# Layer 2's first map by seven products in seven of sixteen groups, with the norm prepared three groups ahead

## The chip, the core and the metric

The kernel runs on one core of one Trainium2 chip. The core has TensorE (matrix products), VectorE, ScalarE and POOL (GpSimd) for elementwise work, and queues for DMA, most of them issued by SyncE (SP). The engines run side by side and wait for each other through semaphores. The metric is the device time of one execution in microseconds (us). The kernel before takes 2445.6 us, the median of three runs (2445.13, 2445.6 and 2445.6).

## What is computed

The input x has 128 batches of 64 nodes with 256 features, in float32. Four layers follow one another, each of the form x = x + f(relu(layernorm(x))). Layer 0 is a graph convolution with LSTMs, layer 1 an attention under the graph's mask, layer 3 three graph convolutions. The change is in layer 2:

```
    h = jnp.maximum(_layernorm(x, axis=-1), 0.0)
    ...
        agg = jnp.einsum('nm,bmd->bnd', A_hat, features)
        x = agg.reshape(-1, d)
        h = jax.nn.relu(_batchnorm(x @ W1.T + b1, g1, be1))
        out = h @ W2.T + b2
        out = _batchnorm(out, g2, be2)
```

The 64 nodes are mixed by a 64 x 64 matrix, a first map takes 256 features to 512, a normalization over all 8192 tokens follows, then a relu, a second map from 512 to 256 and another normalization. A normalization over all tokens needs every group's statistics before it can be applied to the first group. A bias that is added ahead of it moves the mean and nothing else.

## The kernel before

The 8192 tokens are cut into 16 groups (g = 0 to 15) of 512 tokens; a tile of a group has 128 partitions. In layer 2 every group owns an "arena", a tile of four slots of 128 x 512. Slots 0 and 1 first hold the normed and rectified tokens (`activated`, L812), tokens along the partitions. `mixed` (L818, helper `mix`, matmuls at L145) mixes the nodes by 64 x 64 matmuls, which also turn the tile, so that slots 2 and 3 hold 256 features by 512 tokens. `hidden` (L822) is the first map: for each of four blocks m of 128 outputs two matmuls (L831) over the two feature blocks into one bank of PSUM, statistics of the result on VectorE (L842, tile `st1`), and a copy with the bias added on ScalarE (L843) into slot m. As m = 2 and 3 are written last, they overwrite the map's own operand.

PSUM has eight banks, given out in turn by `bank`; a mix takes two, a first map four. An engine takes its instructions in the order of the program that a planner writes; `tc.issue_after` puts instructions behind a named one in that order.

Around the loop at L1137 the order is this. The end of attention (L1083 to L1097) already does groups 0 and 1 in part, with the mixes of 0 and 1. Then step g, for g from 2 on, norms group g+1 (statistics L92, aggregates L94, the power -1/2 on POOL at L96, the shift on VectorE at L98, four applications on ScalarE at L111, one for each tile of 128 tokens), mixes group g+1 (one copy on ScalarE, one on VectorE, L158), and does the first map of group g. At g = 3 the second map's weights are fetched into columns 512 to 1024 of the attention's weight tile, which layer 1 has left. The first map's weights lie in columns 0 to 512.

After group 15 `bn_finish` (L1106) makes a scale and a shift for each m from the statistics, with one power on POOL for each, and `activate` (L1224) applies them to a group with the relu. The second map then runs for groups 0 to 3 and 13 to 15 with plain matmuls (L1262), and for groups 4 to 12 by seven products (`second_linear`, L1205, matmuls at L1211).

`seven` (L171) is the helper for a product of 2 x 2 blocks by seven instead of eight block products. Sums of the left blocks (`sums`, L218) and differences of the right blocks (`differences`, L209) are made first. Products 1, 5, 6 and 7 go to four banks; ScalarE copies 1 and 5 out (L180, L181), VectorE adds 6 and 7 to them (L183, L184), POOL adds these two for the last block (L188), and products 2, 3 and 4 are added onto banks that have been read:

```
            products[2](ps[0], False)
            end(0, 0, ps[0])
            products[3](ps[1], False)
            nc.vector.tensor_tensor(out[0][1], p1, ps[1], ALU.add)
            end(0, 1, None)
            products[4](ps[3], False)
```

Product 4 goes to the bank that L184 reads. Layers 0, 1 and 3 use the same helper (matmuls at L569, L881, L1419, L1459 and L1507).

Of the kernel before, what the change touches and what calls it, by code (L numbers as in the profile page):

```python
# [14 lines left out]
P = 128  # L15
# [23 lines left out]
def adj_preln_kernel(ctx: ExitStack, tc: tile.TileContext, x_in, adj, vec, bg0, bg1,  # L39
# [770 lines left out]
    h1s = []  # L810

    def activated(pool, g, between=None):  # L812

        a = arena(pool)
        ln_relu(xs[g], a[:, 0:2, :].rearrange("p a (b d) -> p (a b) d", d=D), between)
        h1s.append(a)

# [20 lines left out]
    def hidden_out(g, ms, pss):  # L838
        a = h1s[g]
        counted = []  # L840
        for m, ps in zip(ms, pss):
            counted.append(nc.vector.bn_stats(st1[:, m, g, :], ps))  # L842
            nc.scalar.activation(  # L843
                a[:, m, :], ps, AF.Identity, bias=vecs[:, V_B1 + m : V_B1 + m + 1]
            )
        return counted

# [4 lines left out]
    with tc.tile_pool(name="att", bufs=2, reuse_waits="tile") as ap_:  # L852
        shifts_made = []

        def normalized(g):
            h = ap_.tile([P, GT, D], F32, tag="h", name="h")
            st, mv, rstd, nmr = (
                lnp.tile([P, GT] + n, F32, tag=t, name=t)
                for t, n in (("st", [6]), ("mv", [2]), ("rstd", []), ("nmr", []))
            )  # L860
            for t in range(GT):
                nc.vector.bn_stats(st[:, t, :], xs[g][:, t, :])
            for t in range(GT):
                nc.vector.bn_aggr(mv[:, t, :], st[:, t, :])
            nc.vector.tensor_scalar(rstd, mv[:, :, 1], LN_EPS, None, ALU.add)
            nc.gpsimd.tensor_tensor(out=rstd, in0=rstd, in1=mhalf, op=ALU.pow)
            nc.vector.tensor_scalar(nmr, mv[:, :, 0], -1.0, None, ALU.mult)
            shifts_made.append(nc.gpsimd.tensor_tensor(out=nmr, in0=nmr, in1=rstd, op=ALU.mult).ins)
            ln_apply(xs[g], h, rstd, nmr)
            return h  # L870
# [114 lines left out]
        def add_output(g, pss, ri):  # L985
            xv = xs[g].rearrange("p t (m q d) -> p (t m) q d", m=2, q=2)
            for par in range(2):
# [4 lines left out]
                nc.gpsimd.tensor_tensor(out=xv[:, :, par, :], in0=xv[:, :, par, :], in1=o, op=ALU.add)  # L992
# [91 lines left out]
        with tc.issue_after(sub):  # L1084
            counted = hidden(0, w1, range(2))
            mixed(1, (on_scalar, on_scalar))
            pss_0 = hidden_products(0, w1, range(2, 4))
# [3 lines left out]
        with tc.issue_after(turned):  # L1091
            ln_apply(xs[2], h1s[2][:, 0:2, :].rearrange("p a (b d) -> p (a b) d", d=D), rstd, nmr)
            counted += hidden_out(0, range(2, 4), pss_0)
        sums_of()
        counted_next = hidden(1, w1, range(2))
# [10 lines left out]
    def bn_finish(st, n, v_0, v_g, v_b, tag, biased=True):  # L1106


        scs, shs = [], []
        for m in range(n):  # L1110
# [11 lines left out]
            if not biased:  # L1122
                nc.vector.tensor_tensor(mean, mean, vecs[:, v_0 + m : v_0 + m + 1], ALU.add)
# [6 lines left out]
            scs.append(sc)  # L1130
            shs.append(sh)
# [4 lines left out]
    behind = [[], [], counted]  # L1136
    for g in range(1, NG):  # L1137
        if g == 1:
            mixed_in = mixed(2, (on_scalar, on_scalar))
            behind.append(counted_next + hidden(1, w1, range(2, 4)))  # L1140
            continue
        if g + 1 < NG:
            with tc.issue_after(behind[g - 1][-1].ins if behind[g - 1] else after_attention):
                pool = ar_right if g + 1 < NG // 2 else keep if g + 1 == NG // 2 else ar_left
                with tc.issue_after(mixed_in):
                    activated(pool, g + 1, (lambda: behind[g][1]) if behind[g] else None)
                mixed(g + 1, (on_scalar, on_vector))
        if g == 3:
            for a in range(2):
                nc.sync.dma_start(  # L1150
                    out=w2[a], in_=w2t.rearrange("(a b p) f -> a p b f", a=2, p=P)[a]
                )
        behind.append(hidden(g, w1))
# [520 lines left out]
```

## Time and profile before

| | |
|---|---|
| median of three runs | 2445.6 us |
| the profiled execution | 2446.36 us |
| its span, first to last instruction | 2444.5 us |
| TensorE busy | 2425.3 us, 99% |
| VectorE, ScalarE, POOL busy | 1539.8, 1127.5, 463.9 us |
| first map L831, 16 groups | 1430.4 us to about 1565 us of the span |
| one step of a group in the middle of the loop | 8.15 us |
| second map by seven products L1211, 9 groups | 54.4 us |

The profile is one execution. A row of a group of instructions gives line, engine, operation, output and inputs, shapes, how many, then the busy time and the mean duration of one in ns, then the idle time of the engine ahead of them and what ended it. A float32 matmul shows as two records, called passes here, each with its own weight load (PEld). The chain is the work that ended last, followed back from the end; in order of time each line is a start, a length and what ran. Durations contain the latency of an instruction, so that two in a row take less than twice one.

### The profile page before, as it was taken

The numbers are of one execution on the slowest core, as the hardware profiler recorded it, in microseconds if no ns is written. First come the engines' busy times: TensorE is split into PE (matmuls) and PEld (weight loads), VectorE is DVE, ScalarE is ACT, GpSimd is POOL, SyncE is SP. The second block draws the span as 40 slices with busy tenths as digits, with TensorE's granted clock in tenths as the row PEclk, the third lists the DMA queues.
The fourth block names the chain that finished last, engine by engine and source line by source line (L and its number), as shares of the span: only waits on it lengthen the run. The fifth ranks groups of instructions, "written<-read, shape, count | busy, mean of one in ns | idle before, by whom it ended". The sixth has DMA issues, their size and how long they took to land.

```text
span 2444.5 us, 46563 instructions
## 1 busy us (share of the span) xinstructions
PE 2425.3 (99%) x19564; PEld 2068.5 (85%) x19564; DVE 1539.8 (63%) x2752; ACT 1127.5 (46%) x2010; POOL 463.9 (19%) x400
## 2 busy tenths in 40 slices
PE   9999999999999999999999999999999999999999
PEld 6678888889999998888888864486988898898888
DVE  6668866666566675575599886476556445454544
ACT  4557754544444443353455566564333323333332
POOL 4432211111111111112224431023111111101110
PEclk9999999999999999999999999999999999999999
DMA  3200000001000000143246410010133100000000
GB/s 128 94 2 1 1 18 1 1 1 35 1 1 1 1 1 1 18 96 70 48 81 128 79 36 2 1 61 10 29 60 62 27 10 19 10 10 10 18 10 18
DMA packets 161585, 73.20 MB, mean 30 GB/s; under 512 B 104416, under 2 KB 157792, under 8 KB 161376
## 3 DMA queue, kind: packets, MB, share of 16 engines
q1 hardware_dynamic: 147712, 56.82, 9.5%
q0 software_dynamic: 12672, 12.58, 3.4%
q8 instruction: 154, 2.52, 0.4%
q10 hardware_dynamic: 992, 0.82, 0.1%
q14 instruction: 55, 0.45, 0.1%
HBM read 40.84 MB, written 20.97 MB: 25 GB/s over the span
## 4 chain that ended last, share of the span: by engine, by line
PE 91%; DVE 5%; ACT 2%; issue 1%; DMA 0%; POOL 0%; DVEq 0%; ACTq 0%; POOLq 0%
PE ps L569 41%; PE ps L1459 16%; PE ps L1507 8%; PE ps L831 4%; PE ps L1419 4%; PE ps L145 4%; PE ps L881 3%; PE ps L512 2%; PE ps L488 2%; PE ps L1211 2%; PE ps L1262 2%; PE ps L903 1%; PE ps L1528 1%; PE ps L964 1%; DVE e L947 1%
## 5 line engine op out<-in xcount | busy, mean ns | idle before, releaser
L569 PE MATMUL ps<-diff,s 128*128 128x256 f32 (+1 forms) x1824 | 393.5, 371 | 0.9 <-DVE diff L690 0.9
L1459 PE MATMUL ps<-arena 128*128 128x256 f32 x1792 | 393.3, 380 | 0.3 <-DVE arena L215 0.3
L1459 PEld LDWEIGHTS ps<-arena 128*128 128x128 f32 x1792 | 337.9, 190 | 55.1 <-issue 9.8
L569 PEld LDWEIGHTS ps<-diff,s 128*128 128x128 f32 x1824 | 345.9, 190 | 33.8 <-issue 1.6
L583 ACT ACTIVATE gates<-gates,lbias 128x512 f32<-128x512 f32 (+5 forms) x426 | 244.3, 621 | 200.5 <-DVE gates L194 144.4
L188 POOL TENSOR_TENSOR gates<-p 128x512 f32<-128x512 f32 (+1 forms) x115 | 148.6, 1292 | 882.0 <-DVE p L184 831.1
L569 PE MATMUL ps<-h,w 128*128 128x256 f32 (+1 forms) x1028 | 241.0, 371 | 0.0
L569 PE MATMUL ps<-diff,w 128*128 128x256 f32 (+1 forms) x1040 | 238.7, 370 | 0.0
L569 PEld LDWEIGHTS ps<-diff,w 128*128 128x128 f32 x1040 | 197.4, 190 | 18.2
L569 PEld LDWEIGHTS ps<-h,w 128*128 128x128 f32 x1028 | 195.0, 190 | 19.2 <-issue 0.5
L583 ACT ACTIVATE gates<-ps,lbias 128x256 f32<-128x256 f32 (+3 forms) x213 | 91.9, 477 | 247.5 <-PE ps L569 247.4
L188 POOL TENSOR_TENSOR arena<-arena 128x256 f32<-128x256 f32 (+1 forms) x73 | 82.2, 1126 | 579.0 <-DVE arena L184 549.3
L238 ACT ACTIVATE arena<-arena 128x512 f32<-128x512 f32 x144 | 88.1, 627 | 187.0 <-POOL arena L188 95.0
L1507 PE MATMUL ps<-arena 128*128 128x128 f32 x1280 | 149.7, 276 | 0.0
L194 DVE TENSOR_TENSOR gates<-p,ps 128x512 f32<-128x512 f32 (+1 forms) x115 | 76.4, 664 | 114.4 <-PE ps L569 114.2
L1507 PEld LDWEIGHTS ps<-arena 128*128 128x128 f32 x1280 | 145.5, 192 | 1.1
L194 DVE TENSOR_TENSOR arena<-arena,ps 128x256 f32<-128x256 f32 (+1 forms) x73 | 43.6, 597 | 156.2 <-PE ps L1459 87.4
L183 DVE TENSOR_TENSOR p<-p,ps 128x512 f32<-128x512 f32 (+1 forms) x131 | 86.9, 663 | 47.9 <-PE ps L569 46.7
L569 PE MATMUL ps<-state,w 128*128 128x256 f32 (+1 forms) x512 | 116.1, 370 | 0.9 <-ACT p L180 0.8
L198 DVE TENSOR_TENSOR gates<-p,ps 128x512 f32<-128x512 f32 (+1 forms) x115 | 76.6, 666 | 63.3 <-PE ps L569 62.7
L831 PE MATMUL ps<-arena,w 128*128 128x512 f32 x256 | 116.0, 606 | 0.0
L569 PE MATMUL ps<-state,s 128*128 128x256 f32 (+1 forms) x512 | 115.8, 369 | 0.0
(207 smaller groups left out, 4012.0 us busy)
## 6 DMA issues: line engine op xcount, KB each, us to landing
x<-in_x SPq DMA_DIRECT2D x19, 512.0 KB, 4.2
y<-turned SPq DMA_DIRECT2D x64, 128.0 KB, 3.6
v<-vt SPq DMA_DIRECT2D x128, 64.0 KB, 2.3
w<-in_wih SPq DMA_DIRECT2D x4, 1024.0 KB, 7.6
x_for_h<-in_x SPq DMA_DIRECT2D x8, 512.0 KB, 7.1
x<-y POOLq DMA_DIRECT2D x8, 512.0 KB, 6.3
x_for_h<-y POOLq DMA_DIRECT2D x8, 512.0 KB, 6.7
z<-w SPq DMA_DIRECT2D x64, 64.0 KB, 2.0
```

The lines of the kernel that those rows point to most:

```text
L145: last = nc.tensor.matmul(pss[b][half * 64 : half * 64 + 64, c, t, :], lhsT=src[rows, t, col : col + 64], rhs=a2[rows, :], start=True, sto ...
L183: nc.vector.tensor_tensor(p1, p1, ps[2], ALU.add)
L188: nc.gpsimd.tensor_tensor(out=out[1][1], in0=p1, in1=p5, op=ALU.add).ins
L194: nc.vector.tensor_tensor(out[0][1], p1, ps[1], ALU.add)
L198: last = nc.vector.tensor_tensor(to, p, q, ALU.add)
L238: nc.scalar.activation(o, o, func)
L569: nc.tensor.matmul(ps[:, r], lhsT=wc[:, j, :], rhs=bc, start=first and r == 0 and c == 0, stop=True, skip_group_check=True,)
L583: nc.scalar.activation(o, ps, func, bias=lbias[:, col : col + 1])
L831: nc.tensor.matmul(ps, lhsT=w1[:, c, m * P : (m + 1) * P], rhs=a[:, 2 + c, :], start=(c == 0), stop=(c == 1),)
L1419: nc.tensor.matmul(ps[:, t, :], lhsT=w[:, t * P : (t + 1) * P], rhs=b, start=first and t == 0, stop=True, skip_group_check=True,)
L1459: nc.tensor.matmul(ps[:, r, :], lhsT=w[:, c, col : col + P], rhs=b[:, c, :], start=first and r == 0 and c == 0, stop=c == 1, skip_group_ch ...
L1507: nc.tensor.matmul(ps[:, t, :], lhsT=w[:, c, t * P : (t + 1) * P], rhs=b[:, c, :], start=first and t == 0 and c == 0, stop=c == 3, skip_gr ...
```

## The change

- Groups 3, 4, 6, 7, 9, 10 and 12 make their first map by seven products (`hidden_seven`), blocks of 256 outputs by 256 features by 256 tokens. The sums of the weight blocks are made once on POOL, behind the last addition of attention, into the columns that the second weights will take; the differences of the mixed features are made by POOL for each of these groups, one step ahead, in two halves of one more arena. The statistics of these groups are taken from the copied result in SBUF.
- The second map's weights are fetched at g = 13, behind the last group of seven products.
- The norm is split: statistics and scale of group g+3 in step g (`scale`), with the shift on POOL (`ln_on_pool`, moved out of attention's `normalized`), and the application of group g+2 in step g (`rectified`), behind the first copies of step g. Group 3's application stands behind the copy of group 1's m = 0.
- Plain groups go through m in the order 2, 3, 0, 1 and write m into slot (m + 2) mod 4, so slots 0 and 1 (the normed tokens, already mixed) are written first. What reads the slots later, the relu, the second map and its blocks, follows this; `bn_finish` goes through m in this order.
- A seven group's mix is copied twice by ScalarE.
- The first map's bias is no longer added by ScalarE; `bn_finish` adds one more small VectorE operation for each m, as it did for the second normalization.

```diff
@@ -807,13 +807,37 @@
...
-    h1s = []
-    def activated(pool, g, between=None):
+    h1s, evicted = [], []
+    FREE_FIRST = (2, 3, 0, 1)
+    def slot(m):
+        return (m + 2) % 4
+    def ln_on_pool(src):
+        st, mv, rstd, nmr = (
+            lnp.tile([P, GT] + n, F32, tag=t, name=t)
+            for t, n in (("st", [6]), ("mv", [2]), ("rstd", []), ("nmr", []))
+        )
+        for t in range(GT):
+            nc.vector.bn_stats(st[:, t, :], src[:, t, :])
+        for t in range(GT):
+            nc.vector.bn_aggr(mv[:, t, :], st[:, t, :])
+        nc.vector.tensor_scalar(rstd, mv[:, :, 1], LN_EPS, None, ALU.add)
+        nc.gpsimd.tensor_tensor(out=rstd, in0=rstd, in1=mhalf, op=ALU.pow)
+        nc.vector.tensor_scalar(nmr, mv[:, :, 0], -1.0, None, ALU.mult)
+        last = nc.gpsimd.tensor_tensor(out=nmr, in0=nmr, in1=rstd, op=ALU.mult)
+        return rstd, nmr, last.ins
+    def activated(pool, g, between=None, scaled=None):
-        ln_relu(xs[g], a[:, 0:2, :].rearrange("p a (b d) -> p (a b) d", d=D), between)
+        dst = a[:, 0:2, :].rearrange("p a (b d) -> p (a b) d", d=D)
+        if scaled:
+            return ln_apply(xs[g], dst, *scaled)
+        ln_relu(xs[g], dst, between)
@@ -840,33 +864,57 @@
...
-            nc.scalar.activation(
-                a[:, m, :], ps, AF.Identity, bias=vecs[:, V_B1 + m : V_B1 + m + 1]
-            )
+            evicted.append(nc.scalar.copy(a[:, slot(m), :], ps).ins)
+    def hidden_differences(g, ts):
+        a = h1s[g]
+        flat = a.rearrange("p c n -> p (c n)")
+        first = flat[:, 2 * GN : 3 * GN].rearrange("p (i n) -> p i n", n=HN)
+        nc.gpsimd.tensor_tensor(out=ts[:, 0:3:2], in0=a[:, 2:4, HN:], in1=first, op=ALU.subtract)
+        nc.gpsimd.tensor_tensor(out=ts[:, 1], in0=a[:, 3, HN:], in1=ts[:, 0], op=ALU.subtract)
+        nc.gpsimd.tensor_tensor(out=ts[:, 3], in0=a[:, 3, 0:HN], in1=ts[:, 1], op=ALU.subtract)
+    def hidden_seven(g, w, ts, copied, added):
+        a = h1s[g]
+        out = [[a[:, 2 - 2 * m : 4 - 2 * m, n * HN : (n + 1) * HN] for n in range(2)] for m in range(2)]
+        b = [[a[:, 2 + c, n * HN : (n + 1) * HN] for n in range(2)] for c in range(2)]
+        def product(wb, x):
+            def issue(ps, first):
+                for r in range(2):
+                    nc.tensor.matmul(
+                        ps[:, r, :], lhsT=wb[:, r * P : (r + 1) * P], rhs=x,
+                        start=first and r == 0, stop=True, skip_group_check=True,
+                    )
+            return issue
+        finish = seven(
+            sevens(w, (*b, [ts[:, i] for i in range(4)]), product),
+            [bank((P, 2, HN)) for _ in range(4)],
+            out[1][0], out[1][1], out, ends_in(out, AF.Copy),
+        )
+        with tc.issue_after(finish.copied):
+            copied()
+        added(finish.behind)
+        finish()
+        return [nc.vector.bn_stats(st1[:, m, g, :], a[:, slot(m), :]) for m in range(4)]
...
         def normalized(g):
...
+            rstd, nmr, made = ln_on_pool(xs[g])
...
@@ -1082,17 +1133,17 @@
-            counted = hidden(0, w1, range(2))
+            counted = hidden(0, w1, range(2, 4))
-            pss_0 = hidden_products(0, w1, range(2, 4))
+            pss_0 = hidden_products(0, w1, range(2))
-            counted += hidden_out(0, range(2, 4), pss_0)
+            counted += hidden_out(0, range(2), pss_0)
-        counted_next = hidden(1, w1, range(2))
+        counted = hidden(1, w1, range(2, 4))
...
-    def bn_finish(st, n, v_0, v_g, v_b, tag, biased=True):
-        scs, shs = [], []
-        for m in range(n):
+    def bn_finish(st, ms, v_0, v_g, v_b, tag):
+        scs, shs = {}, {}
+        for m in ms:
-            if not biased:
-                nc.vector.tensor_tensor(mean, mean, vecs[:, v_0 + m : v_0 + m + 1], ALU.add)
+            nc.vector.tensor_tensor(mean, mean, vecs[:, v_0 + m : v_0 + m + 1], ALU.add)
-            scs.append(sc)
-            shs.append(sh)
+            scs[m], shs[m] = sc, sh
-    behind = [[], [], counted]
+    SEVEN_FC1 = (3, 4, 6, 7, 9, 10, 12)
+    fc1_a = [[w1[:, c, m * D : (m + 1) * D] for c in range(2)] for m in range(2)]
+    fc1_s = [
+        w_att[:, i // 2, 512 + i % 2 * D : 512 + (i % 2 + 1) * D] for i in range(4)
+    ]
+    with tc.issue_after(outputs_added[-1]):
+        sums(nc.gpsimd, *fc1_a[0], *fc1_a[1], *fc1_s)
+    fc1_w = (*fc1_a, fc1_s)
+    fc1_ts = arena(ar_left).rearrange("p i (h n) -> p (i h) n", n=HN)
+    def fc1_t(g):
+        i = SEVEN_FC1.index(g) % 2
+        return fc1_ts[:, 4 * i : 4 * i + 4]
+    counted = [None, counted]
+    scaled = {}
+    def scale(n, behind):
+        if n < NG:
+            with tc.issue_after(behind):
+                scaled[n] = ln_on_pool(xs[n])[:2]
+    def rectified(n):
+        if n < NG:
+            pool = ar_right if n < NG // 2 else keep if n == NG // 2 else ar_left
+            return activated(pool, n, scaled=scaled[n])
+    scale(3, after_attention)
     for g in range(1, NG):
         if g == 1:
-            mixed_in = mixed(2, (on_scalar, on_scalar))
-            behind.append(counted_next + hidden(1, w1, range(2, 4)))
-            continue
-        if g + 1 < NG:
-            with tc.issue_after(behind[g - 1][-1].ins if behind[g - 1] else after_attention):
-                pool = ar_right if g + 1 < NG // 2 else keep if g + 1 == NG // 2 else ar_left
-                with tc.issue_after(mixed_in):
-                    activated(pool, g + 1, (lambda: behind[g][1]) if behind[g] else None)
-                mixed(g + 1, (on_scalar, on_vector))
-        if g == 3:
-            for a in range(2):
-                nc.sync.dma_start(
-                    out=w2[a], in_=w2t.rearrange("(a b p) f -> a p b f", a=2, p=P)[a]
+            mixed(2, (on_scalar, on_scalar))
+            counted[1] += hidden(1, w1, range(2))
+        else:
+            if g + 1 < NG:
+                seven_next = g + 1 in SEVEN_FC1
+                mixed(g + 1, (on_scalar, on_scalar if seven_next else on_vector))
+                if seven_next:
+                    hidden_differences(g + 1, fc1_t(g + 1))
+            if g == SEVEN_FC1[-1] + 1:
+                for a in range(2):
+                    nc.sync.dma_start(
+                        out=w2[a], in_=w2t.rearrange("(a b p) f -> a p b f", a=2, p=P)[a]
+                    )
+            if g in SEVEN_FC1:
+                counted.append(
+                    hidden_seven(
+                        g, fc1_w, fc1_t(g), lambda: rectified(g + 2), lambda last: scale(g + 3, last)
+                    )
-        behind.append(hidden(g, w1))
+                continue
+            pss = hidden_products(g, w1, FREE_FIRST)
+            counted.append(hidden_out(g, FREE_FIRST[:1], pss))
+            with tc.issue_after(evicted[-1]):
+                last = rectified(g + 2)
+            with tc.issue_after(last) if last else nullcontext():
+                counted[g] += hidden_out(g, FREE_FIRST[1:], pss[1:])
+        scale(g + 3, counted[g][2 if g == 1 else 0].ins)
+        if g == 1:
+            with tc.issue_after(evicted[-2]):
+                rectified(3)
-    sc1, sh1 = bn_finish(st1, 4, V_B1, V_G1, V_BE1, "n1")
+    sc1, sh1 = bn_finish(st1, FREE_FIRST, V_B1, V_G1, V_BE1, "n1")
...
-            order = [(c, m) for c in range(4) for m in range(2)]
+            order = [(c, m) for c in FREE_FIRST for m in range(2)]
-                    pss[m], lhsT=w2[c // 2][:, c % 2, m * P : (m + 1) * P], rhs=a[:, c, :],
-                    start=(c == 0), stop=(c == 3),
+                    pss[m], lhsT=w2[c // 2][:, c % 2, m * P : (m + 1) * P], rhs=a[:, slot(c), :],
+                    start=(c == FREE_FIRST[0]), stop=(c == FREE_FIRST[3]),
-            def evicted(m):
+            def evict(m):
...
```

More of the change, by code (lines that the diff above doesn't have):

```diff
@@ L852, in adj_preln_kernel @@
     with tc.tile_pool(name="att", bufs=2, reuse_waits="tile") as ap_:
-        shifts_made = []
+        shifts_made, outputs_added = [], []
         def normalized(g):
             h = ap_.tile([P, GT, D], F32, tag="h", name="h")
[L857 to L868, printed above, removed]
+            rstd, nmr, made = ln_on_pool(xs[g])
             ln_apply(xs[g], h, rstd, nmr)
+            shifts_made.append(made)
             return h
@@ L991, in add_output @@
                 )
-                nc.gpsimd.tensor_tensor(out=xv[:, :, par, :], in0=xv[:, :, par, :], in1=o, op=ALU.add)
+                added = nc.gpsimd.tensor_tensor(
+                    out=xv[:, :, par, :], in0=xv[:, :, par, :], in1=o, op=ALU.add
+                )
+            outputs_added.append(added.ins)
             return last
@@ L1148, in adj_preln_kernel @@
-        if g == 3:
-            for a in range(2):
-                nc.sync.dma_start(
-                    out=w2[a], in_=w2t.rearrange("(a b p) f -> a p b f", a=2, p=P)[a]
-                )
-        behind.append(hidden(g, w1))
+            mixed(2, (on_scalar, on_scalar))
[15 more added lines that the diff above has]
+                        g, fc1_w, fc1_t(g), lambda: rectified(g + 2), lambda last: scale(g + 3, last)
+                    )
+                )
+                continue
[5 more added lines that the diff above has]
+                counted[g] += hidden_out(g, FREE_FIRST[1:], pss[1:])
@@ L1193, in fc2_blocks @@
         return [
-            [a[:, 2 * c : 2 * c + 2, n * HN : (n + 1) * HN] for n in range(2)] for c in range(2)
+            [a[:, 2 - 2 * c : 4 - 2 * c, n * HN : (n + 1) * HN] for n in range(2)]
+            for c in range(2)
         ]
@@ L1220, in second_linear @@
             sevens((*fc2_a, fc2_s), (*fc2_blocks(a), ts), product), [bank((P, HN)) for _ in range(4)],
-            a[:, 0, HN:], a[:, 1, HN:], blocks, ends_in(blocks, AF.Copy),
+            a[:, 2, HN:], a[:, 3, HN:], blocks, ends_in(blocks, AF.Copy),
         )
@@ L1225, in activate @@
         a = h1s[g]
-        for m in range(4):
+        for m in FREE_FIRST:
             nc.scalar.activation(
-                a[:, m, :], a[:, m, :], AF.Relu,
+                a[:, slot(m), :], a[:, slot(m), :], AF.Relu,
                 bias=sh1[m], scale=sc1[m],
@@ L1272, in adj_preln_kernel @@
                 if (g, m) != (NG - 1, 1):
-                    last = evicted(m)
+                    last = evict(m)
             if g + 2 < NG:
@@ L1280, in adj_preln_kernel @@
             w_three = layer3_weights()
-    sc2, sh2 = bn_finish(st2, 2, V_B2, V_G2, V_BE2, "n2", biased=False)
+    sc2, sh2 = bn_finish(st2, range(2), V_B2, V_G2, V_BE2, "n2")
     b1, t1s, a2, s2s, b3, t3s = w_three
@@ L1383, in first_start @@
             normalize(g, chunks=[1], on_scalar=range(2))
-        evicted(1)
+        evict(1)
         lns = []
```

## The prediction

> **What bounds the kernel now.** I read the page's busy row and chain first, then the chain in order of time through layer 2, then TensorE's timeline and the stretches where it is not full, then the groups of the other engines.
>
> ```profile
> PE 2425.3 (99%) x19564; PEld 2068.5 (85%) x19564; DVE 1539.8 (63%) x2752; ACT 1127.5 (46%) x2010; POOL 463.9 (19%) x400
> ...
> PE 91%; DVE 5%; ACT 2%; issue 1%; DMA 0%; POOL 0%; DVEq 0%; ACTq 0%; POOLq 0%
> ```
>
> TensorE sets the end almost everywhere; a TensorE pass removed is a gain only if nothing else becomes late. The chain through the stage that changes (start, length, what):
>
> ```profile
> 1493.23 1.09 PE ps L145 x64
> 1494.32 7.06 PE ps L831 x16
> 1501.39 1.09 PE ps L145 x64
> 1502.48 7.06 PE ps L831 x16
> ...
> 1593.78 54.40 PE ps L1211 x252
> ```
>
> Each group is a mix (L145, 1.09) and the first map (L831, 7.06, 16 passes: eight fp32 matmuls, two records each). A period is 8.155 us, and from 1461 to 1551 nothing but TensorE is on the chain. L1211 is layer 2's second map, already by seven products: nine groups in 54.40 us, 6.04 a group. The entry to the stage is different (first TensorE's timeline, then the stretches around it, with the busy time of TensorE, of its weight loads, of VectorE, ScalarE and POOL; the third figure from the end is the granted clock, 1.00 at full speed):
>
> ```profile
> 1445.14 3.70 PE L831 MATMUL ps<-arena,w 128*128 128x512 f32 x8
> 1449.92 1.92 PE L145 MATMUL ps<-ah,arena 64*64 64x64 f32 x64 [1.09 <-ACT arena L111]
> 1451.78 8.83 PE L831 MATMUL ps<-arena,w 128*128 128x512 f32 x16
> ```
>
> ```profile
> 1443.00:1449.00 6.00, 5.84 (x137) 3.40 (x136) 5.71 (x23) 3.92 (x8) 1.02 (x1) 1.00 0.01 3
> 1449.00:1455.00 6.00, 5.00 (x69) 2.65 (x70) 4.75 (x16) 4.83 (x10) 3.50 (x3) 0.77 0.01 3
> 1455.00:1461.00 6.00, 6.00 (x42) 2.66 (x44) 2.71 (x7) 4.77 (x10) 1.02 (x1) 0.95 0.00 1
> ```
>
> TensorE waits 1.09 us for the norm of group 3 on ScalarE, runs the mix in 1.92 instead of 1.16 because the norm's four tiles come one by one, and then the clock falls: group 2's map takes 8.83 instead of 7.13. Together 3.6 us.
>
> **The change, part by part.**
>
> *Seven products for seven groups (3, 4, 6, 7, 9, 10, 12).* A plain group is 16 passes of 512 columns; their weight loads stand 0.43 apart, so 16 x 0.43 = 6.88, and 0.18 of the 7.06 goes where TensorE changes between 64-row and 128-row tiles. A group of seven is 14 matmuls of 256 columns, 28 passes. The same shape runs in L1211 at 54.40 / 252 = 0.2159 a pass: 28 x 0.2159 = 6.04. With all 0.18 of the tile change kept it is 6.22, with none 6.04; layer 3's L1419 (28 passes of 256 columns) takes 6.13 up to a 64-row matmul. I take 6.18, 0.14 of change. Saved: 7.06 - 6.18 = 0.88 a group, 7 x 0.88 = 6.2 us (ends 5.9 and 7.1).
>
> [...] A load is 190 ns here: 16 x 0.19 = 3.0 of 7.06 us (43%) before, 28 x 0.19 = 5.3 of 6.18 (86%) after. [...] were the loads not hidden, the worst I would allow is the saving gone, 6.2 us lost. The row decides: L1211 holds 0.2159 a pass with loads at 88% (47.8 of 54.4 us).
>
> *Is what surrounds it covered?* The step of a seven group is then 1.09 + 6.18 = 7.27. VectorE in it: four norm statistics (1.39 for x4, 1.31 to the next), four aggregates 0.28, two small ones 0.3, four additions from PSUM and four statistics of 512 columns. The rows of these, with latency:
>
> ```profile
> L842 DVE BATCH_NORM_STATS2 st<-ps 128x6 f32<-128x512 f32 x64 | 44.4, 697 | 43.0 <-PE ps L831 42.4
> ...
> L194 DVE TENSOR_TENSOR arena<-arena,ps 128x512 f32<-128x512 f32 x18 | 12.4, 688 | 38.6 <-PE ps L1459 32.8 <-PE ps L1419 5.9
> ...
> L1254 DVE BATCH_NORM_STATS2 st<-arena 128x6 f32<-128x512 f32 x18 | 12.2, 689 | 0.8
> ```
>
> Two in a row show 1.28 to 1.29, 0.60 each: 8 x 0.60 = 4.8. Sum 1.3 + 0.3 + 0.3 + 4.8 = 6.7, and 0.6 for the mix's copy where a plain group follows: 7.3 against 7.27. A plain step needs 1.9 + 4 x 0.60 = 4.3 against 8.16 and lets it catch up. Three steps (seven, seven, plain): 6.7 + 7.3 + 4.3 = 18.3 of 22.7. Within a pair the tight point is product 4 of the second group, which needs the addition at L184 done. Count from that step's start T. VectorE still holds the first group's last addition (product 4 of it ends at T, so T+0.2 to 0.8), its four statistics (to 3.2) and the copy (3.8). L183 to 4.4; L184 must await product 7 (T+1.2+4 x 0.86 = 4.6) and ends at 5.3. Product 4 is due at T+6.3: 1.0 us spare. ScalarE: four norm tiles 2.0, two copies of the mix 1.1, three of products 1.6, 4.7 of 7.27. POOL: power 1.02, shift 0.20 (the row of the same operation in attention), differences 1.28 + 2 x 0.95 (rows L188 and L215), addition 1.28: 5.7 of 7.27, and the differences are made a whole step ahead, with about 3 us to spare. No stall in steady state, so cost 0.
>
> *Norm steps ahead.* The statistics go to three groups ahead, the norm itself to two, the shift from VectorE to POOL. In the steady state the norm was not late before, so this is worth nothing there. At the entry it is. VectorE's order in the changed program is: statistics of group 3 (as before, 1444.1), aggregates, two statistics of group 1, both attention outputs (2 x 0.60), then group 1's m=0 statistics, at about 1448.3 to 1449.0. ScalarE's copy of that result now stands ahead of group 3's norm (before, the norm started at 1449.25 right behind the mix's copies): copy 1449.05 to 1449.55, first norm tile done at 1450.15. TensorE stands from 1448.84 to 1450.2: 1.35 instead of 1.09. The fourth tile follows a second copy and is done at 1452.1; but one matmul of group 2 now fills the wait for it (TensorE's order puts it between the mix's third and fourth tile). Mix plus that matmul end at 1452.7; before, the same work ended at 1451.84 + 0.86 = 1452.7. Net 0. POOL must make the four weight sums (4 x 0.95) behind attention's last additions (to 1450.3) and ahead of group 4's power: 1454.1 + 1.0 + 0.2 = 1455.4; group 4's norm is due on ScalarE at about 1456.9. Covered by 1.5; if that cover goes, the norm of group 4 has a further 3 us before TensorE's mix.
>
> The clock at the entry: [...] The row shows the clock at 0.77 after a wait of only 1.09 (plus three gaps between tiles). I go by the row: same 1.7 as before, net 0; -1.7 stays as the lower end and +1.7 (a second slow stretch, of the same size) as the upper.
>
> *Free slots first, no bias in the first map.* The copy 0.58 replaces the activation 0.68 on ScalarE, off the path: 0. The second weights now load behind group 12 instead of group 3, on SP; they have two steps (16 us) for two 256 KB transfers (1 MB loads land in 7.6): 0. The first normalization gains one VectorE addition for each of four m, behind the wait for POOL's power. This chain is on the path:
>
> ```profile
> 1567.81 0.62 DVE st L842
> 1568.45 0.60 DVE n1mv L1114
> ...
> 1570.07 0.23 DVE n1sh L1126
> 1570.33 0.82 ACT arena L1227
> ```
>
> In the second normalization, which has that addition, it adds 0.08 between its neighbours. 4 x 0.06 to 0.08 = 0.25 us more before the last activation; TensorE's wait there grows from 0.51 to 0.76 (ends 0 and 0.6).
>
> *Sum.* -6.2 + 0 + 0.25 = -5.95. The profiled execution is 2446.36 with a span of 2444.5: 2440.4 and 2438.55 after. The runs' median stands 0.76 below the profiled time: 2445.6 - 5.95 = 2439.65.
>
> **Rivals.**
>
> *VectorE becomes the bound and the kernel slower.* In the seven groups it goes from 62% (5.1 of 8.15 in one group's stretch) to 92%. For: 17 dependent instructions a step[...]. Against: 1.0 us spare at product 4, and a plain group follows each pair. It decides when VectorE's part of a step passes 7.27 by 0.88, at 8.15 us, which is 22% above my sum. If it came so late that each of the seven groups stood 1.0 us and paid the clock as at the entry, 7 x (1.0 + 1.7) - 5.95 = +13: 2458.5.
>
> *Part of it is given back.* One or two stalls in the three pairs, or at the first seven group, which starts right after the slow stretch; 1.0 us with the clock's 1.7 once: 2442.3. For: the clock's fall after 1.09 us. Against: the spare times above.
>
> *The entry keeps its clock.* 2439.65 - 1.7 = 2438.0. For: [...] that the mix's gap is filled. Against: a longer first wait.
>
> *The change does nothing.* Loads not hidden behind 256 columns: 2445.6 + 0.25 = 2445.8. L1211 speaks against.
>
> **How the numbers follow.** Likeliest (net of the sum) 0.58, 2439.65, its own range 2438.0 to 2441.0: the ends of its terms (-7.1 and -5.3), widened by 0.5 and 0.7 for the entry. Given back in part 0.20. Entry keeps its clock 0.10. Nothing 0.05. Slower 0.07. The 0.2% bound, about what a measurement of this kernel can tell from no change, is 4.9 us: 2440.7 and 2450.5. Likeliest lies below 2440.7 for 0.52 of its 0.58; with 0.10 and 0.02 of the partial case: faster 0.64, same 0.29, slower 0.07. The range 2437.2 to 2443.4 leaves out half of "nothing" upward, all of "slower" and the tails.
>
> **What would show it.** Right: the product line in the first map has 196 passes in 7 x 6.2 us; the step of a seven group is 7.2 to 7.3; TensorE has no idle time at product 4; the clock falls once, near 1450; the last activation of the first normalization follows the group's end by 0.2 more. Wrong: waits of TensorE on L184's addition or on POOL's differences, a clock below 1.00 between 1461 and 1545, or an entry more than 1 us later than before at the end of group 2 (1460.6).

## The result, and the profile after

The changed kernel takes 2441.26 us (median of 22 runs, 2439.79 to 2443.13), the kernel before 2445.16 us beside it (22 runs, 2443.99 to 2446.73): ratio 0.9983, interval 0.9978 to 0.9989. That is 3.9 us or 0.16% faster, a real gain, but under the 0.2% that the prediction called measurable. It lies inside the predicted range, 1.6 us above the predicted time and just above the likeliest case's own range (2438.0 to 2441.0): of the 5.95 us forecast a third is missing. The profiled executions show more: 2446.36 and 2441.49 us, spans 2444.5 and 2439.7. What they show is told first, and then why it is not the usual difference.

The busy row and the chain by engine, from the page of the changed kernel:

```profile
PE 2419.9 (99%) x19648; PEld 2084.9 (85%) x19648; DVE 1552.0 (64%) x2777; ACT 1121.7 (46%) x2010; POOL 497.5 (20%) x445
...
PE 92%; DVE 5%; ACT 2%; issue 1%; POOL 0%; DMA 0%; ACTq 0%; DVEq 0%; POOLq 0%
```

TensorE still sets the end; it does 84 more passes and is busy 5.4 us less (1.7 us of this is the clock of one execution, below). The chain of the changed kernel in order of time, in the middle of the stage (start, length, what):

```profile
1482.42 1.09 PE ps L145 x64
1483.51 6.24 PE ps L888 x28
1489.75 1.09 PE ps L145 x64
1490.84 6.24 PE ps L888 x28
1497.08 1.09 PE ps L145 x64
1498.17 7.06 PE ps L855 x16
```

A group by seven products (L888) takes 6.24 where a plain one (now L855) takes 7.06; nothing but TensorE is on the chain. The only waits of TensorE from 1430 to 1570 us are at the entry and behind the first normalization:

```profile
PE ps L145 <- ACT arena L111: 1.4, 1, 1.4
PE ps L1354 <- ACT arena L1319: 0.6, 1, 0.6
```

The entry, first TensorE's timeline (in brackets the wait ahead and whose result ended it) and then the stretches around it (the third figure from the end is the granted clock):

```profile
1445.43 3.70 PE L855 MATMUL ps<-arena,w 128*128 128x512 f32 x8
1450.50 1.45 PE L145 MATMUL ps<-ah,arena 64*64 64x64 f32 x48 [1.37 <-ACT arena L111]
1451.87 1.12 PE L855 MATMUL ps<-arena,w 128*128 128x512 f32 x2
1452.93 0.46 PE L145 MATMUL ps<-ah,arena 64*64 64x64 f32 x16
1453.32 6.28 PE L855 MATMUL ps<-arena,w 128*128 128x512 f32 x14
```

```profile
1443.00:1449.00 6.00, 6.00 (x138) 3.39 (x136) 5.97 (x18) 4.06 (x9) 1.94 (x3) 1.00 0.01 3
1449.00:1455.00 6.00, 4.57 (x71) 2.46 (x71) 4.30 (x13) 4.25 (x9) 5.71 (x9) 1.00 0.01 3
1455.00:1461.00 6.00, 6.00 (x77) 3.09 (x76) 4.21 (x14) 4.24 (x9) 3.94 (x5) 1.00 0.00 1
```

TensorE waits 1.37 us, 0.28 longer than before, and one matmul of group 2 (two passes) stands between the mix's third and fourth tile, all as forecast; but the clock stays at 1.00 where before it fell to 0.77. VectorE's rows in the stage, from 1461 to 1545 us:

```profile
L904 DVE BATCH_NORM_STATS2 st<-arena 128x6 f32<-128x512 f32 x28 | 17.3, 679 | 0.0
...
L184 DVE TENSOR_TENSOR arena<-arena,ps 128x512 f32<-128x512 f32 x7 | 4.8, 689 | 1.0 <-PE ps L888 0.7
```

At L184, the tight point of the prediction, it is VectorE that waits for TensorE and not the other way; in every group by seven L184 ends 0.77 us before product 4 starts. The end of the first normalization on the chain:

```profile
1561.24 0.62 DVE st L866
1561.88 0.60 DVE n1mv L1165
1562.51 0.17 DVE n1sc L1166
1562.74 0.56 POOL n1sc L1167
1563.32 0.16 DVE n1sc L1174
1563.48 0.08 DVE n1mv L1173
1563.59 0.23 DVE n1sh L1176
1563.84 0.82 ACT arena L1319
```

The added operation is the 0.08 at L1173, four times. From the last product on the chain to the last activation it was 10.12 us before (1560.21 to 1570.33) and is 10.40 (1553.44 to 1563.84).

### The profile page after: what moved, and what is told of

Read it like the earlier page. It is cut to its first block, busy times and chain, and to the rows that moved or that the text cites. A ratio compares the mean times of both kernels' runs of the same rounds, so it can differ in the third digit from the quotient of the medians.

```text
span 2439.7 us, 46858 instructions
## 1 busy us (share of the span) xinstructions
PE 2419.9 (99%) x19648; PEld 2084.9 (85%) x19648; DVE 1552.0 (64%) x2777; ACT 1121.7 (46%) x2010; POOL 497.5 (20%) x445
## 4 chain that ended last, share of the span: by engine, by line
PE 92%; DVE 5%; ACT 2%; issue 1%; POOL 0%; DMA 0%; ACTq 0%; DVEq 0%; POOLq 0%
PE ps L569 41%; PE ps L1551 16%; PE ps L1599 8%; PE ps L145 4%; PE ps L1511 4%; PE ps L929 3%; PE ps L512 2%; PE ps L488 2%; PE ps L1303 2%; PE ps L855 2%; PE ps L888 2%; PE ps L1354 2%; PE ps L951 1%; PE ps L1620 1%; PE ps L1012 1%
## 5 line engine op out<-in xcount | busy, mean ns | idle before, releaser
L1551 PE MATMUL ps<-arena 128*128 128x256 f32 x1792 | 393.4, 381 | 0.4 <-issue 0.4
L1551 PEld LDWEIGHTS ps<-arena 128*128 128x128 f32 x1792 | 337.8, 190 | 55.4 <-issue 10.8
L188 POOL TENSOR_TENSOR arena<-arena 128x512 f32<-128x512 f32 (+1 forms) x80 | 90.8, 1134 | 598.5 <-DVE arena L184 598.5
L194 DVE TENSOR_TENSOR arena<-arena,ps 128x512 f32<-128x512 f32 (+1 forms) x80 | 48.1, 602 | 155.5 <-PE ps L1551 87.4
L183 DVE TENSOR_TENSOR arena<-arena,ps 128x512 f32<-128x512 f32 (+1 forms) x80 | 48.1, 602 | 106.7 <-PE ps L1551 53.5
```

What stands on the lines that cost most here:

```text
L183: nc.vector.tensor_tensor(p1, p1, ps[2], ALU.add)
L188: nc.gpsimd.tensor_tensor(out=out[1][1], in0=p1, in1=p5, op=ALU.add).ins
L1551: nc.tensor.matmul(ps[:, r, :], lhsT=w[:, c, col : col + P], rhs=b[:, c, :], start=first and r == 0 and c == 0, stop=c == 1, skip_group_ch ...
```

## Theory and rivals

To find the missing third I cut every trace at the same points of TensorE's timeline: the *stage*, from the first map's first product to the end of the 12 second-map passes that run ahead of TensorE's wait for the normalization; the second map's nine groups of sevens; and *layer 3*, from its first product at L1459 (changed kernel L1551) to the start of TensorE's last group. The starting point of the stage itself moves by up to 2.5 us between runs (1430.3 to 1432.8), so lengths are compared and not times of day.

The first runs ask about the clock. Theory A: its fall in the first profile of the kernel before (8.83 instead of 7.13) was an accident of that execution; theory B: it belongs to every run of that kernel. The later ones ask where the rest went. My theory: the sevens give what they seem to give; the rest of the change costs something at the entry and at the normalization, and something is lost far behind the stage. Rivals: the sevens save less than they seem to, because something else becomes late, or VectorE is nearly the bound.

## The experiments

**Both kernels once more.**

> The kernel before, unchanged, profiled a second time. Its first profiled execution (2446.36) lay 1.2 above its median of 22 runs (2445.16), and lost 1.7 us to a fallen clock in group 2's map. Theory A, the fallen clock at the entry is a matter of luck and the usual run doesn't have it: group 2's map takes about 7.1 instead of 8.8 us, and the time is near 2444.7. Theory B, the entry always loses the clock after its wait of 1.09: 8.8 again.

> The changed kernel, unchanged, profiled a second time. In its first profile the wait at the entry was 1.37 us and the clock was kept (group 2's map 1.12 + 6.28 for 16 passes). Theory A: kept or lost by luck; if lost, group 2's map and mix end some 1.7 us later. Theory B': the changed entry keeps it always because a matmul fills the mix's last gap: the same as in the first profile. Steps of seven groups 7.33 us both ways.

Measured 2445.49 and 2441.06 us. TensorE's timeline of the kernel before, second profile:

```profile
1450.67 1.93 PE L145 MATMUL ps<-ah,arena 64*64 64x64 f32 x64 [1.08 <-ACT arena L111]
1452.53 7.13 PE L831 MATMUL ps<-arena,w 128*128 128x512 f32 x16
```

The same wait, the same gaps between tiles, and no fall: 7.13 instead of 8.83. The 1.7 us of the first profile is not in this execution, whose time lies at the median, so B falls as an "always"; the fall came again in a later profile (six small matmuls, below). The changed kernel repeats its first profile: a wait of 1.38 us, the clock kept. With the clock kept on both sides the stage is 138.55 before and 133.39 after, 5.16 less. The table has the lengths of all runs in us, by the starts and ends in TensorE's timeline. The stage runs from the first product of the first map to the end of the 12 passes of the second map ahead of the wait for the normalization (for instance 1558.41 + 5.72 - 1430.74 = 133.39), layer 3 from the first L1551 (before: L1459) to the start of the last row of L1620 (before: L1528):

| run | stage | second map, sevens | layer 3 | median |
|---|---|---|---|---|
| before, first profile | 140.24 | 54.56 | 746.65 | 2445.16 |
| before, again | 138.55 | 54.56 | 746.72 | |
| before, wait filled | 138.55 | 54.56 | 746.72 | 2444.94 |
| before, 6 small matmuls | 140.24 | 54.56 | 748.55 | 2447.11 |
| after, first profile | 133.39 | 54.94 | 746.91 | 2441.26 |
| after, again | 133.39 | 54.94 | 747.42 | |
| after, wait filled | 133.74 | 54.95 | 748.52 | 2442.78 |
| after, 3 small matmuls | 133.39 | 54.95 | 746.39 | 2440.52 |
| no sevens | 139.16 | 54.94 | 746.39 | 2446.14 |
| ten sevens | 130.92 | 54.95 | 746.03 | 2437.71 |
| norm of group 3 earlier | 132.46 | 54.94 | 747.30 | 2439.64 |
| statistics twice | 142.39 | 54.94 | 746.40 | 2448.76 |
| eleven sevens, norm earlier | 130.78 | 54.93 | 746.02 | 2436.24 |
| ten sevens, norm earlier | 129.99 | 54.94 | 745.95 | 2436.39 |

**The wait at the entry filled with a matmul**, in both kernels (a first product made twice, for m = 3 before and m = 1 after):

```diff
-            for c in range(2):
+            for c in (0, 0, 1) if (g, m) == (1, 3) else range(2):
...
```

> The kernel before, with one matmul of group 1's last block (m = 3) made twice, 0.86 us of TensorE work put into its wait at the entry. The wait falls from 1.09 to about 0.2. Theory A: if the usual run of before doesn't lose the clock, the median stays within 0.4 us of before. Theory B: the clock is no longer lost and the median falls by 1.5 to 1.7 us.

> The changed kernel with the same extra matmul (group 1's m = 1). The wait falls from 1.37 to about 0.5. If the longer wait of the changed entry costs its usual run the clock (a rival for where 2 us of the forecast went), the median falls by 1.5 us from 2441.3, to about 2439.7; if the usual run keeps the clock, it stays at 2441.3 within 0.4.

Measured 2444.94 us before (ratio 1.0, 0.9991 to 1.0008) and 2442.78 after (0.999, 0.9982 to 0.9998, against the kernel before). In the kernel before TensorE's wait falls from 1.08 to 0.22 and its stage stays at 138.55: the extra matmul exactly takes the wait's place, and the clock is kept. Its median lies only 0.38 us under that of the kernel before beside it (2445.32, 25 runs). If the usual run lost the clock, the fill would have taken 1.5 to 1.7 us out. So theory A holds: the usual run of the kernel before keeps its clock. In the changed kernel the fill made it 1.5 us *slower*, which neither side of the expectation had: two waits at the entry (0.54 and 0.26, stage +0.35), and layer 3, over 200 us further on and untouched, took 1.1 to 1.6 us longer. That was the first sign of a cost that no part of the change accounts for.

**Without the sevens; with ten of them.**

```diff
-    SEVEN_FC1 = (3, 4, 6, 7, 9, 10, 12)
+    SEVEN_FC1 = ()                        # one run, without the weight sums on POOL
+    SEVEN_FC1 = tuple(range(3, 13))       # the other
```

> The changed kernel with no group by seven products: all fourteen later groups plain, the rest of the change (norm steps three groups ahead, outputs in the slots that are free first, bias left to the batch norm) kept. Theory (the sevens save 0.82 us each on TensorE, and the rest of the change costs about 1 us): 7 x 0.82 = 5.8 us more than the changed kernel, 2447.0 (2446.3 to 2447.7), slower than the kernel before by 1 to 2 us; each step of the stage 8.15 us. Rival (the sevens save less than they seem to, since something else waits): 2442 to 2444.5.

> The changed kernel with ten groups by seven products, 3 to 12, with no plain group between. Theory (TensorE bounds the step at 7.33 us, VectorE at some 6.7 fits under it): three more steps of 7.33 instead of 8.15, 2.5 us less than the changed kernel, 2438.8 (2438.0 to 2439.5), no wait of TensorE inside the stage. Rival (VectorE or the buffers bound sevens that follow one another): waits of TensorE ahead of a mix or inside the products, 0.5 us or more per step, 2441 to 2445.

Measured 2446.14 us (ratio 1.0004, 0.9996 to 1.0012) and 2437.71 (0.9967, 0.9955 to 0.998). The stage is 5.77 longer without sevens and 2.47 shorter with three more: 0.82 a group both ways, as in the chain. Ten in a row run with no wait of TensorE between them; VectorE is busy 6.74 to 6.75 of each step, the 6.7 of the prediction's sum (three successive steps; VectorE is the third of the engine figures):

```profile
1475.00:1482.33 7.33, 7.33 (x93) 6.26 (x92) 6.74 (x19) 4.82 (x9) 5.23 (x6) 1.00 0.01 2
1482.33:1489.67 7.34, 7.34 (x94) 6.27 (x93) 6.75 (x19) 4.82 (x9) 5.23 (x6) 1.00 0.01 2
1489.67:1497.00 7.33, 7.33 (x94) 6.26 (x93) 6.75 (x19) 4.82 (x9) 5.24 (x6) 1.00 0.00 0
```

The first rival falls. Both times are about 1 us under the expectation and just outside its range; both runs have a shorter layer 3 (746.39 and 746.03). The run without sevens also prices the rest of the change in the stage: 139.16 - 138.55 = 0.61 us *lost*.

**VectorE loaded.** The four statistics of a seven group are made twice.

```diff
         finish()
+        for m in range(4):
+            nc.vector.bn_stats(st1[:, m, g, :], a[:, slot(m), :])
         return [nc.vector.bn_stats(st1[:, m, g, :], a[:, slot(m), :]) for m in range(4)]
```

> The changed kernel with the four batch statistics of each group by seven products made twice (2.7 us more on VectorE in each of seven groups). Theory (TensorE bounds a pair and the plain group behind it at 22.8 us; VectorE has 18.3 us of work in them, which becomes 23.7): TensorE waits 0.9 us or more per pair, more where a buffer is held, up to 1.9 us per seven: 2444 to 2454, with waits whose releaser is VectorE. Rival (VectorE isn't near the bound): less than 1 us more, 2442.2 or under.

Measured 2448.76 us (ratio 1.0016, 1.0009 to 1.0022), the stage 9.0 longer. TensorE's waits in the stage:

```profile
PE ps L888 <- DVE arena L184: 3.1, 3, 1.0
PE ps L145 <- ACT arena L111: 2.5, 5, 1.4
```

```profile
1473.16 0.45 PE L145 MATMUL ps<-ah,arena 64*64 64x64 f32 x12
1474.64 1.10 PE L888 MATMUL ps<-arena,w 128*128 128x256 f32 x4 [1.03 <-DVE arena L184]
```

(from the list of waits, us in total, times, longest; and TensorE's timeline). TensorE stops where the prediction put the tight point: product 4 of the second group of a pair, behind L184, in each of the three pairs. The second set of statistics takes 2.46 us; with the 1.0 spare of the prediction product 4 should come 1.46 late. It starts 6.85 us behind the group's first product (1467.79 to 1474.64), in the changed kernel 5.29 (1467.95 to 1473.24), so it comes 1.56 late, and a part of the mix fills 0.45 of that. The place was right, and the spare time is 0.9 instead of 1.0. A pair and its plain group now take 25.47 us instead of 22.82. The rival's deciding point, 8.15 us of VectorE in the step of a group by seven, is passed (6.7 + 2.5 = 9.2), and the gain is indeed gone: three plain steps take 24.5 us. Over the three steps, though, VectorE has only 18.3 + 2 x 2.5 = 23.3 us of work; an average over them would not have shown the loss. Of the 2.65 us a pair, 1.03 is this wait, 0.29 and 0.77 go where the next norm is late and its tiles come to the mix one by one, and the rest with the split mix. What counts is the latest product, not the sum.

**Where the code lies.** A few 64 x 64 matmuls in the wait at the very start, 64 being the smallest operand that the kernel already uses. Their result is used by nothing; they move TensorE's later instructions within the pieces, 154 of 16.4 KB each, that the page's queue of instructions brings (q8, below). At the start they take 0.69 us for three and 1.34 for six (4.33 to 5.67 in the timeline), more than the expectations say.

```diff
             keep_busy(7)
+            for _ in range(3):                 # 6 in the kernel before
+                nc.tensor.matmul(idle[0:64, 0:64], lhsT=ones[0:64, 0:64], rhs=ones[0:64, 0:64],
+                                 start=True, stop=True)
```

> The changed kernel with three matmuls of 64 x 64 more in the wait at the very start (12 instructions of TensorE, some 0.1 us, in time it waits in anyway). Theory (the waits without a releaser in layer 3, 0.5 us in the third step and 0 to 0.4 in the eleventh, fall where TensorE's instructions cross from one 16 KB piece of code to the next): the pieces now end elsewhere in the steps, these waits go or move, layer 3 from its first product to TensorE's last instruction takes 746.5 us or less instead of 746.9 to 747.4, the time is 2440.2 to 2440.9. Rival (the waits belong to the program's own semaphores): they stay at the same matmuls, 2441.0 to 2441.5.

> The kernel before with six matmuls of 64 x 64 more in the wait at the very start (24 instructions of TensorE, some 0.15 us). Theory of code pieces: this puts the ends of the pieces where they fall in the changed kernel with one extra matmul, which lost 1.9 us in layer 3: layer 3 from its first product to the last instruction of TensorE takes 747.7 to 748.7 us instead of 746.7, with waits without a releaser just behind the small products, the time is 1 to 2 us longer, 2446.2 to 2447.2. Rival: layer 3 as before, 2445.2.

Measured 2440.52 us for the changed kernel (ratio to the kernel before 0.9982, 0.9974 to 0.999) and 2447.11 for the one before (1.0008, 1.0 to 1.0016). Layer 3 is 746.39 and 748.55, both as the theory of code pieces had them: three matmuls at the start took 0.5 to 1.0 us out of the changed kernel's layer 3, and six put 1.8 us into the other's. The chains of the changed kernel (again) and of the kernel before with six small matmuls:

```profile
1778.71 1.90 PE ps L145 x128
1780.61 0.43 PE ps L1620 x8
1781.04 0.84 PE ps L1551 x3
1781.89 0.42 issue
1782.31 1.78 PE ps L1551 x7
```

```profile
1833.99 1.73 PE ps L145 x116
1835.71 0.43 PE ps L1533 x8
1836.15 0.41 PE ps L1464
1836.56 0.77 issue
1837.33 4.69 PE ps L1464 x21
```

"issue" is time in which TensorE waited for nothing that the profile shows. The queue that brings its instructions is, by its count, this one in the page's list of queues (transfers, MB, share), kernel before:

```profile
q8 instruction: 154, 2.52, 0.4%
```

2.52 MB in 154 transfers are 16.4 KB each; in the trace every one has 16384 bytes. TensorE has 39442 instructions in the trace (19564 loads, as many matmuls, 314 others), in the changed kernel 39623 to 155 transfers: 256 to a transfer and 64 bytes each, an estimate by division (256.1 and 255.6). I counted TensorE's instructions up to each load in layer 3 that came late without a releaser: 27073 and 34497 in the changed kernel; 27073, 29889, 34497 and 37313 with the wait filled; 27842 and 35266 in the kernel before with six small matmuls; 32450 without the sevens. Each leaves 193 or 194 when divided by 256. With the filled wait the program is four instructions longer, and the stall stayed at 27073, two passes earlier in layer 3's program. So it belongs to the place in the stream and not to the instruction. That TensorE waits there for its next piece is what the counts point to; no record of the trace names what ended the stall. (In both profiles with small matmuls the stage also began 1 to 2 us later than in most others. With six, two more such stalls stand ahead of it, 0.65 and 0.93 us at 1249.6 and 1308.5, at 194 behind a multiple of 256; with three the delay lies ahead of layer 0's long products.) All in layer 3 stand behind a mix of 128 small passes, which uses up 256 instructions in 1.9 us; 256 instructions of the sevens last 128 x 0.2159 = 27.6 us.

**The norm of group 3 earlier on ScalarE**: straight behind the copies of group 2's mix instead of behind the eviction of group 1's m = 0.

```diff
-            mixed(2, (on_scalar, on_scalar))
+            mixed_2 = mixed(2, (on_scalar, on_scalar))
+            with tc.issue_after(mixed_2):
+                rectified(3)
...
-        if g == 1:
-            with tc.issue_after(evicted[-2]):
-                rectified(3)
```

> The changed kernel with the norm of group 3 given to ScalarE straight behind the copies of group 2's mix, ahead of the eviction that it stood behind. Theory (the entry costs 0.4 us more than before because ScalarE comes to group 2's tiles 0.3 us later, and because a matmul group is put between the mix tiles): TensorE waits 0.9 to 1.1 us at the entry instead of 1.37, stage from its first product to the end of the first map 133.0 instead of 133.4 us; time 2440.4 to 2441.2. Rival (the clock: with the mix tiles together again the fall seen in two profiles of the kernel before comes back): group 2's products take 8.8 us instead of 7.1, stage 134.7.

Measured 2439.64 us (ratio 0.9977, 0.9968 to 0.9986). TensorE's entry:

```profile
1450.28 1.93 PE L145 MATMUL ps<-ah,arena 64*64 64x64 f32 x64 [0.56 <-ACT arena L111]
1452.13 7.13 PE L855 MATMUL ps<-arena,w 128*128 128x512 f32 x16
```

The wait falls to 0.56, below the kernel before, and the planner leaves the mix in one piece; the stage is 0.93 shorter, twice what I expected, and the clock is kept. The changed kernel's entry was late because of one eviction ahead of the norm.

**Together.**

> The changed kernel with eleven groups by seven products, 3 to 13, and the norm of group 3 given to ScalarE straight behind the copies of group 2's mix, ahead of the eviction that it stood behind. Theory: four more sevens save 4 x 0.82 = 3.3 us, and the wait at the entry falls from 1.37 to about 0.9 us: some 3.7 us less than the changed kernel, 2437.5, with layer 3 between 747.3 and 749.8 us by where the code pieces end: 2436.6 to 2438.6. Rival (VectorE at 6.75 us of a step of 7.33 falls behind over eleven steps, or the clock falls at the entry, 1.7 us): waits of TensorE inside the stage, or the first map 1.7 us longer; 2438.6 to 2441.

> The changed kernel with ten groups by seven products, 3 to 12, and the norm of group 3 given to ScalarE straight behind the copies of group 2's mix. Theory (the two gains add, and the late norm of the last group, which made TensorE wait 1.6 us behind the eleventh, stays away): stage from its first product to the end of the first map 133.4 - 0.9 - 2.5 = 130.0 us, no wait of TensorE in it but the 0.56 us at the entry, layer 3 747.3 us as in the runs with ten and eleven; time 2435.5 to 2437.0. Rival (they share a gain, or the wait behind the last one comes with ten as well): stage 130.8 us or more, 2437 or more.

Measured 2436.24 us (ratio 0.9963, 0.995 to 0.9975) and 2436.39 (0.9961, 0.9948 to 0.9975). With eleven, the norm of group 15 comes late and TensorE waits 0.75 us ahead of the last mix, which then takes 1.94 instead of 1.16: the stage is 130.78 where the gains sum to 132.46 - 4 x 0.82 = 129.2. With ten the two gains add to 129.99, as expected. In medians the two can't be told apart; both beat the changed kernel by some 5 us and the kernel before by 0.4%.

## Why the prediction was right and where not

With the clock kept on both sides the lengths account for the gain: stage -5.16, wait behind the normalization +0.07, second map +0.38, layer 3 +0.19 to +0.70. Sum -4.5 to -4.0, beside -3.9 of the medians. Of the 2.05 us that the forecast is short by, 0.43 are the sevens (5.77 instead of 6.2), 0.39 the entry, 0.03 the normalization, 0.38 the second map and 0.19 to 0.70 layer 3.

- *Seven products, 0.88 a group, 6.2 us.* Right in mechanism, a little large. A group takes 6.24 and not 6.18: all of the tile change is kept (6.24 - 6.04 = 0.20), where I had taken 0.14. 7.06 - 6.24 = 0.82; seven times this, 5.77 by the run without sevens, lies just under the lower end of 5.9. 28 loads of 190 ns are 85% of 6.24 us, and in the stage no product of L888 waited for anything; so the row (L1211) and not the load's busy share was the right judge.
- *Is what surrounds it covered.* Right. No wait of TensorE between 1461 and 1544; 6.7 us of VectorE was measured at 6.75, and the 1.0 us spare came out at 0.9 in the loaded run. POOL's sums took 2.92 for four, less than the 3.8 of the estimate.
- *Norm steps ahead, net 0 at the entry.* Wrong by 0.39. The wait grew to 1.37 as forecast (1.35). But I set "mix plus that matmul" equal on both sides with the matmul at 0.86; set between the mix's tiles it has a change of tile shape on either side, and takes 1.06 (1451.87 to 1452.93). From the stage's start to the end of group 2 it is 28.40 before (again) and 28.79 after.
- *The clock at the entry, "same 1.7 as before".* Wrong in this: the row of one execution was taken for the kernel's habit. Its net of 0 for the clock held by luck, because the usual run loses it on neither side. The fall was there in two of three profiles of the kernel before with the wait of 1.08 to 1.09 us, and in none of six of the changed kind with 1.37 or 1.38, so the length of the wait doesn't decide. Its place may. The changes of the clock stand whole multiples of 3.4133 us apart in the traces: in the first profile of the kernel before at 4.97, 1452.22 and 1455.63 us (424 steps and one), in the first of the changed kernel at 9.80 and 2436.68 (711 steps). The program's start lies differently on this grid in the two: 4.97 and 9.80 are 1.4 steps apart. The steps of the grid at the entry, with the products of the first map alone (busy time of TensorE, of its loads, then the clock): the first profile of the kernel before, the step behind it, and the second profile.

```profile
1448.81:1452.22 3.41, 0.47 (x2) 0.30 (x2) 1.00 0.00 0
1452.22:1455.63 3.41, 3.41 (x5) 1.35 (x4) 0.50 0.03 5
1449.73:1453.14 3.41, 0.61 (x2) 0.37 (x3) 1.00 0.00 0
```

In both profiles with the fall (the first, and the one with six small matmuls) one step holds the whole wait and the whole mix, and 0.47 us of products. In the second profile the step begins 0.14 us after the wait does and has 0.61 us; in the six of the changed kind the emptiest has 0.92, all of it the matmul between the tiles. Wait and mix together take 2.94 us, so by these lengths about one position in seven would hold them whole (an estimate, (3.41 - 2.94) / 3.41). That is not far from the 12 of 120 runs of the kernel before that lie more than 1 us above their median, but no run varied the position, so the place is a likely cause and not a shown one. The first profiles' 4.8 us of span are then -5.16 in the stage and -1.69 of clock, +0.71 behind the stage, +0.29 by which the stage began later and +1.08 by which the last output landed later behind TensorE's end.
- *End of the first normalization, +0.25.* Right: +0.28, but only 0.07 of it is in the wait (0.51 to 0.58); 0.21 is in the 12 passes ahead, which wait for single activations (5.51 to 5.72).
- *Behind the stage.* The sum had nothing there; this is the step that failed. Second map: +0.38, in every kernel of the changed kind, with sevens or without. ScalarE's order at the start of the nine groups, changed kernel (again), timeline:

```profile
1587.89 0.58 ACT L1360 COPY arena<-ps 128x512 f32<-128x512 f32 x1 [3.30 <-DVE st L1363]
1588.37 0.38 ACT L180 COPY arena<-ps 128x256 f32<-128x256 f32 x1
1588.64 0.60 ACT L1360 COPY arena<-ps 128x512 f32<-128x512 f32 x1
1589.11 2.94 ACT L1319 ACTIVATE arena<-arena,n1sh,n1sc 128x512 f32<-128x512 f32 x4
```

The copy of a product (L180) has come between the two evictions; before, it stood behind them and the four activations. The loads behind the last activations wait 0.21 and 0.40. Why the planner changed it was not tried. Layer 3: TensorE's program has 168 loads and matmuls and 13 waits more by then, and by the theory of code pieces these end at other places of the steps: 0.53 more was measured in the third step in both profiles and 0.45 in the eleventh in one. In the last step L184 on VectorE runs 0.35 late though the products that it reads are done at the same point. The kernel before has two longer steps of its own, by some 0.3 each, so that +0.19 to +0.70 remain. The late L184 is in all five profiles with the changed kernel's 3569 VectorE instructions, where it stands 191 behind a multiple of 256, and in none of the nine with other counts; VectorE's own code is the likely cause, which is argued and not shown.

Of the rivals, "part of it is given back" came nearest in time (2442.3), but by another mechanism: no wait in the pairs. "The entry keeps its clock" described the first profiles and not the medians, since the usual run of the kernel before keeps it too. "The change does nothing" falls with the 6.24 us of a group.

Open: what makes the clock fall at the entry in some executions and not in others; why the planner moved the copy in the second map; and the kernel without the added bias operation, which was not run.

## What to carry to other kernels

Take a slow stretch of one profile into a sum only if a second profile of the same kernel shows it; cut traces at the same points of the bounding engine and compare lengths. When an engine has slack in a step by its sum, look for the one product that waits for it: the spare time there was forecast to 0.1 us, while a sum over a pair and its plain group hides the wait. An edit that changes the number of TensorE's instructions can change a stage that it doesn't touch (12 more at the start took 0.5 to 1.0 us out of the changed kernel's layer 3, 24 put 1.8 us into the other's), so a gain of 0.1% is read from the lengths of the stages and not from the median alone.

## What was not expected of the hardware

In layer 3 TensorE stalled, behind a mix of 128 small passes, at places that leave 193 or 194 when its instructions are divided by 256, as many as a transfer of 16.4 KB holds by the estimate above: 0.41 us in the first profile of the changed kernel, 0.77 and 0.85 us in that of the kernel before with six small matmuls. Layer 3 has some 56 such places in the changed kernel (14436 instructions of TensorE), and none to four of them show in a profile. 24 instructions more at the start of the program made layer 3, the program's last third, 1.8 us longer (748.55 instead of 746.72).

The fall of TensorE's clock after a wait of 1.08 to 1.09 us comes and goes between executions of one program: in the first profile of the kernel before it was at 0.50 from 1452.22 to 1455.63 us, in the second group 2's products took 7.13 us instead of 8.83. The traces put its changes on a grid of 3.413 us that is not tied to the program: a step begins 0.02 us ahead of the wait in the first profile and 0.14 behind its start in the second.
